# Copies into the keys' input on VectorE, and scatters tied in pairs to their row-number casts: a change to a two-layer perceiver kernel

## The chip, the cores and the metric

The kernel runs on one core of one Trainium2 chip. The core has five engines that run beside each other, each through its own list of instructions in order: TensorE (PE, matmuls; its weight loads are shown as PEld), VectorE (DVE), ScalarE (ACT), GpSimd (POOL) and SyncE (SP, which here issues transfers). [...] Transfers between memory and the core run on 16 DMA engines.

The metric is the device time of one execution in microseconds (us); lower is better. The kernel before takes 2748.53 us, the median of three runs (2745.07 to 2750.08).

## The reference

Sixty-four sequences of 32 tokens of width 256 (`x`) pass two layers. Each layer has a cross attention to a context of 257 tokens per sequence, a self attention, and a feed-forward part; each part adds its result to `x`. All is float32.

```python
def reference(x, ctx, mask, ...):
    x = x + L0_xattn(ctx, layernorm(x), mask, ...)   # queries from ln; keys and values from [xn ; ln], 257 + 32 of them
    x = x + L0_attn(layernorm(x), ...)
    x = x + L0_ffn(layernorm(x), ...)                # mixture of experts
    x = x + L1_xattn(layernorm(x), ctx, ...)
    x = x + L1_attn(layernorm(x), ...)
    x = x + L1_ffn(layernorm(x), ...)
    return x

def L0_ffn(x):                                       # 2048 tokens, 64 experts, 8 for each token
    w, idx = top_k(softmax(x @ gate_w), 8)           # w is then divided by its sum
    pos = place of each choice in its expert's queue # those from 128 on are dropped
    buf[expert, pos] = x                             # one row of 256 numbers for each choice
    out = experts(buf)                               # two matmuls with a silu gate for each expert
    y = sum over the 8 choices of w * out[expert, pos]
    return y + shared_expert(x)
```

In the first cross attention a sequence's keys come from 289 tokens: the first 256 of its context, then the sequence's own 32 tokens (after their layernorm), then the context's last one.

## The kernel before

The 2048 tokens are 16 tiles of 128, four sequences in each. There are three stages. The first, `before`, loops over the 64 sequences: first cross attention, and for each tile, some sequences later, the self attention and the routing (`tail`). The second, `experts`, first finishes the tails that are left and then goes through the 64 experts. The third, `after`, loops over the sequences again for the second layer.

A scheduler places the instructions of DVE, ACT, POOL and SP by priority and by its own estimate of when inputs are there; PE's order is written out by hand: within `tc.manual_schedule(engines={PE})` PE runs its instructions in the order in which the code emits them. The code interleaves the work by Python generators. Each `slot()` in the loop lets every running generator (`tails` for tiles that are done, `fronts` for queries of tiles to come) go on to its next `yield`. A tile has eleven slots. `pause(n)` is n `yield`s. A `yield` sets where PE's instructions go and with which priority the others are emitted; an engine other than PE may still run an instruction from behind a `yield` as early as its inputs allow.

What the change touches:

- `turn(s)` of `CrossFirst` makes `xT`, the transposed 256 x 289 input of a sequence's keys (two buffers that take turns). PE transposes the context (L1235), ACT copies 256 columns out (L1238), and POOL copies the last 33: 32 columns of the sequence's own tokens from `lnT` (L1239) and one of the context's last token from `xlT` (L1240). `keys(s)` multiplies `xT` by the key weights in 16 matmuls (L180, psA<-xT,wk), copies the results to `kT` (L1263 on ACT, L1265 on DVE) and squares them (L1268). `norms` sums the squares on PE (L1280), `scores` multiplies queries and keys (L1320), and DVE scales the scores (L1330).
- `route(t)` is the end of a tile's tail. DVE finds for each token the eight rows of `buf` into which it goes (`far`, float32, with a number outside `buf` for dropped choices), and casts them to int32 (`fi`, L669). POOL then issues eight scatters (L672): scatter k writes the tile's 128 rows of `z` to the rows in column k of `fi`. The scatters are declared free of each other. After each second one the code has a `yield`, but for the last two tiles.

On POOL the scatters share one list with, among others, the products of queries and their norms (L1184), the mask (L1206 to L1208), the weights of the self attention's queries (L565), the count of rows per expert (L653) and the copies into `xT`. The buffer of `z` is one of two that take turns.

Of the kernel before, what the change touches and what calls it, by code (L numbers as in the profile page):

```python
# [19 lines left out]
S = 32  # L20
NB = P // S
J = 257
JK = J + S
# [10 lines left out]
TOPK = 8  # L34
# [56 lines left out]
def pause(n):  # L91

    for _ in range(n):
        yield
# [7 lines left out]
class Kernel:  # L102
# [511 lines left out]
    def route(self, t, gw):  # L614
        nc = self.nc
        z, zT = yield from self.normed(t)
        nc.sync.dma_start(self.zs[t // GT][:, :, t % GT, :], zT)
        ps = self.bank("psA")
        self.product(
            ps[:, : E + 1],  # L620
            [zT[:, k, :] for k in range(2)],
            [gw[:, k, :] for k in range(2)],
        )

        sgt = self.sgate[:, t : t + 1]
        nc.scalar.activation(sgt, ps[:, E : E + 1], AF.Exp, scale=-1.0)
        nc.vector.tensor_scalar(sgt, sgt, 1.0, None, ALU.add)
        nc.vector.reciprocal(sgt, sgt)
        mx = self.small.tile([P, 1], F32, name="mx1")
        sm = self.small.tile([P, 1], F32, name="sm1")  # L630
        nc.vector.tensor_reduce(mx, ps[:, :E], AX.X, ALU.max, negate=True)
        pr = self.wk.tile([P, E], F32, name="pr")
        nc.scalar.activation(pr, ps[:, :E], AF.Exp, bias=mx, accum_out=sm)
        nc.vector.reciprocal(sm, sm)
        nc.vector.tensor_scalar(pr, pr, sm, None, ALU.mult)
        top = self.small.tile([P, TOPK], F32, name="top")
        nc.vector.max(top, pr)
        sel = self.wk.tile([P, E], F32, name="sel")
        nc.vector.match_replace(sel, top, pr, -1.0)
        nc.vector.tensor_scalar(sel, sel, 0.0, None, ALU.is_lt)  # L640
        tot = self.small.tile([P, 1], F32, name="tot")
        nc.vector.tensor_reduce(tot, top, AX.X, ALU.add)
        nc.vector.reciprocal(tot, tot)
        nc.vector.tensor_scalar(pr, pr, tot, None, ALU.mult)

        yield
        yield

        ps = self.bank("psA")
        self.product(ps[:, :E], [self.tri, self.ones], [sel, self.count])  # L650
        kept = self.wk.tile([P, E], F32, name="kept")
        nc.vector.scalar_tensor_tensor(kept, ps[:, :E], float(CAP), sel, ALU.is_lt, ALU.mult)
        nc.gpsimd.tensor_tensor(self.count, self.count, sel, ALU.add)  # L653
        val = self.wk.tile([P, E], F32, name="val")
        nc.vector.tensor_tensor(val, ps[:, :E], self.slot, ALU.add)
        nc.vector.tensor_tensor(val, val, kept, ALU.mult)
        v8 = self.small.tile([P, TOPK], F32, name="v8")
        nc.vector.max(v8, val)
        junk = self.wk.tile([P, E], F32, name="junk")
        for k in range(TOPK):  # L660
            nc.vector.scalar_tensor_tensor(
                junk, val, v8[:, k : k + 1], pr, ALU.is_equal, ALU.mult, accum_out=self.w8[:, t, k : k + 1]
            )
        nc.vector.tensor_copy(self.idx[:, t, :], v8)
        far = self.small.tile([P, TOPK], F32, name="far")
        nc.vector.tensor_scalar(far, v8, 0.0, FAR, ALU.is_equal, ALU.mult)
        nc.vector.tensor_tensor(far, far, v8, ALU.add)
        fi = self.small.tile([P, TOPK], I32, name="fi")
        nc.vector.tensor_copy(fi, far)  # L669

        for k in range(TOPK):
            d = nc.gpsimd.indirect_dma_start(  # L672
                out=self.buf[:, :],
                out_offset=bass.IndirectOffsetOnAxis(ap=fi[:, k : k + 1], axis=0),
                in_=z[:, 0, :],
                in_offset=None,
                bounds_check=E * CAP,
                oob_is_err=False,
            )
            self.tc.declare_no_dep(d.ins, group="scatter", reason="rows differ")  # L680
            self.tc.add_to_no_dep_group("scatter", d.ins)
            if k % 2 and k < TOPK - 1 and t < self.nt - 2:
                yield

    def experts(self, ctx, slot, tails):
        tc, nc, a = self.tc, self.nc, self.a
# [111 lines left out]
        for _ in range(at):  # L798
            next(side)
        turn(0)  # L800
        turn(1)
        inner(0)
        rest = total - at
        for e in range(E):
            weigh(e + AHEAD)
            fetch(e + 3)
            turn(e + 2)
            while (at - total + rest) * E < rest * e:
                next(side)
                at += 1  # L810
            inner(e + 1)
            outer(e)
            if e == AHEAD:
                self.after_weights()
            if e == 2 * AHEAD:
                self.ffnw = self.ffn_weights(self.w2)
# [319 lines left out]
class CrossFirst:  # L1136
# [88 lines left out]
    def turn(self, s):  # L1225

        k, kp = self.k, self.kp
        nc = k.nc
        t, b = divmod(s, NB)
        lnT, cx = self.own[t][1], self.cx[s]  # L1230
        xT = self.xT[s] = kp.tile([P, 2, JK], F32, name="xT")
        ps = k.bank("psT")
        for c in range(2):
            for j in range(2):
                nc.tensor.transpose(  # L1235
                    ps[:, (2 * c + j) * P : (2 * c + j + 1) * P], cx[:, j, c * P : (c + 1) * P], k.ident
                )
        nc.scalar.copy(xT[:, :, : J - 1], ps.rearrange("p (k j) -> p k j", k=2))  # L1238
        nc.gpsimd.tensor_copy(xT[:, :, J - 1 : JK - 1], lnT[:, :, b * S : (b + 1) * S])  # L1239
        nc.gpsimd.tensor_copy(xT[:, :, JK - 1 :], self.xlT[:, :, s : s + 1])  # L1240

    def keys(self, s):

# [291 lines left out]
```

## Time and profile before

| | |
|---|---|
| median of 3 runs | 2748.53 us |
| the profiled execution's own time | 2806.28 us |
| its span, from the first to the last instruction | 2804.2 us |
| mean granted TensorE clock | 0.986 of full speed |
| DMA | 157.05 MB, 56 GB/s over the span |
| POOL's scatters, L672 | 128, 992 ns each, 127.0 us |
| POOL's gathers, L835 | 128, 1027 ns each, 131.4 us |

The profile is one execution, recorded instruction by instruction. Its page gives each engine's busy time, the costliest groups of instructions and what ended the idle time ahead of them. Views of the trace give more: a timeline lists instructions in order of time, with the start and the length in us, the engine, the line, the operation, what is written and what is read, and in brackets the idle time ahead of it and what ended that. "issue" there means that the engine waited for nothing the profile shows. A wait list sums such idle times by pairs. A table of stretches gives the engines' busy times between two points in time.

### The profile page before, as it was taken

The numbers are of one execution on the slowest core, as the hardware profiler recorded it, in microseconds if no ns is written. First come the engines' busy times: TensorE is split into PE (matmuls) and PEld (weight loads), VectorE is DVE, ScalarE is ACT, GpSimd is POOL, SyncE is SP. The second block draws the span as 40 slices with busy tenths as digits, with TensorE's granted clock in tenths as the row PEclk, the third lists the DMA queues.
The fourth block names the chain that finished last, engine by engine and source line by source line (L and its number), as shares of the span: only waits on it lengthen the run. The fifth ranks groups of instructions, "written<-read, shape, count | busy, mean of one in ns | idle before, by whom it ended". The sixth has DMA issues, their size and how long they took to land. (4 is left out here: it accounts for less than half of the span.)

```text
span 2804.2 us, 59449 instructions
## 1 busy us (share of the span) xinstructions
PE 2651.4 (95%) x23642; PEld 1822.2 (65%) x23642; DVE 1736.5 (62%) x4557; ACT 1235.3 (44%) x3474; POOL 543.6 (19%) x644
## 2 busy tenths in 40 slices
PE   6999999999999999999998899899999999999995
PEld 4566656665666566666665578677777777777763
DVE  6565656665676567657755533556666666666664
ACT  4555555555555545555554233333333333333331
POOL 3110122112211221222021300422222222121001
PEclk9999999999999999999999999999999999999997
DMA  8100001101100000000001487221212222221110
GB/s 267 38 16 14 18 31 33 31 18 31 33 28 19 27 22 20 23 17 19 17 9 48 149 292 260 89 62 52 58 48 58 52 58 58 50 58 46 33 33 7
DMA packets 136088, 157.05 MB, mean 56 GB/s; under 512 B 24024, under 2 KB 118979, under 8 KB 135812
## 3 DMA queue, kind: packets, MB, share of 16 engines
q1 hardware_dynamic: 114308, 119.65, 13.9%
q0 software_dynamic: 12288, 25.21, 3.4%
q10 hardware_dynamic: 9216, 8.39, 0.9%
q8 instruction: 187, 3.06, 0.5%
q14 instruction: 89, 0.73, 0.1%
HBM read 121.63 MB, written 37.75 MB: 57 GB/s over the span
## 5 line engine op out<-in xcount | busy, mean ns | idle before, releaser
L180 PE MATMUL psA<-xT,wk 128*128 128x289 f32 x2048 | 525.5, 412 | 18.3 <-issue 13.7
L180 PEld LDWEIGHTS psA<-xT,wk 128*128 128x128 f32 x2048 | 386.5, 191 | 151.3 <-issue 46.5
L835 POOL DMA_INDIRECT y<-oute,idx x128 | 131.4, 1027 | 641.0 <-DVE x L846 466.3
L234 PE MATMUL psY<-at,cx 128*128 128x512 f32 x512 | 237.1, 606 | 0.0
L180 PE MATMUL psY<-xT,qk 128*128 128x257 f32 x1024 | 233.6, 381 | 0.0
L180 PE MATMUL psA<-at,cx 128*128 128x512 f32 x512 | 233.5, 599 | 0.0
L180 PEld LDWEIGHTS psY<-xT,qk 128*128 128x128 f32 x1024 | 189.9, 190 | 25.1
L1421 ACT ACTIVATE sim<-psY,mx 128x257 f32<-128x257 f32 x256 | 120.8, 476 | 148.7 <-DVE mx L1420 147.8
L234 PEld LDWEIGHTS psY<-at,cx 128*128 128x128 f32 x512 | 92.4, 190 | 122.1 <-issue 98.7
L197 ACT ACTIVATE sim<-sim,mx 128x289 f32<-128x289 f32 x256 | 135.4, 532 | 63.2 <-DVE mx L195 63.0
L180 PEld LDWEIGHTS psA<-at,cx 128*128 128x128 f32 x512 | 93.4, 190 | 96.5 <-issue 83.2
L1268 ACT ACTIVATE sq<-kT 128x1156 f32<-128x1156 f32 x128 | 148.5, 1160 | 11.6 <-DVE kT L1265 10.5
L1263 ACT COPY kT<-psA 128x289 f32<-128x289 f32 x256 | 99.3, 388 | 119.7 <-PE psA L180 117.5
L246 ACT COPY yT<-psY 128x512 f32<-128x512 f32 x128 | 68.7, 589 | 188.9 <-PE psY L244 188.9
L1330 DVE TENSOR_TENSOR sim<-psB,sim 128x289 f32<-128x289 f32 x256 | 100.9, 451 | 81.1 <-PE psA L180 28.9
L672 POOL DMA_INDIRECT buf<-z,fi x128 | 127.0, 992 | 96.9 <-DVE fi L669 56.1
L1265 DVE COPY kT<-psA 128x289 f32<-128x289 f32 x256 | 114.0, 449 | 42.7 <-PE psA L180 42.6
L180 PE MATMUL psY<-yT,wv 128*64 128x128 f32 x2048 | 127.9, 277 | 7.3 <-DVE yT L1451 7.3
L1420 DVE TENSOR_REDUCE mx<-psY 128x1 f32<-128x257 f32 x256 | 101.0, 417 | 52.8 <-PE psY L180 52.6
L180 PEld LDWEIGHTS psY<-yT,wv 128*64 128x64 f32 x2048 | 116.6, 138 | 16.3 <-DVE yT L1451 11.2
L186 DVE TENSOR_TENSOR x<-x,psY 128x256 f32<-128x256 f32 (+1 forms) x80 | 29.2, 365 | 154.0 <-PE psY L180 152.4
L180 PE MATMUL psY<-wo,oT 128*128 128x128 f32 (+1 forms) x768 | 124.2, 315 | 0.0
(262 smaller groups left out, 5014.7 us busy)
## 6 DMA issues: line engine op xcount, KB each, us to landing
cx<-in_ctx SPq DMA_DIRECT2D x128, 256.0 KB
we<-in_m_ew SPq DMA_DIRECT2D x64, 384.0 KB
xT<-in_ctxT SPq DMA_DIRECT2D x64, 257.0 KB
buf<-zero SPq DMA_DIRECT2D x32, 256.0 KB
be<-buf SPq DMA_DIRECT2D x64, 128.0 KB
oute<-oe ACTq DMA_DIRECT2D x64, 128.0 KB
mu<-in_mask SPq DMA_DIRECT2D x16, 128.5 KB
x<-in_x SPq DMA_DIRECT2D x16, 128.0 KB
```

Source lines behind the costliest of these rows:

```text
L180: self.nc.tensor.matmul(ps, lhsT=lhs[i], rhs=rhs[i], start=(i == 0), stop=(i == n - 1))
L197: nc.scalar.activation(sim[:, g, :], sim[:, g, :], AF.Exp, bias=mx[:, g : g + 1], accum_out=sm[:, g : g + 1])
L234: nc.tensor.matmul(ps[kc], lhsT=values[i][:, kc * P : (kc + 1) * P], rhs=at[i], start=(i == 0), stop=(i == n - 1 and tail is None),)
L246: nc.any.tensor_copy(yT[:, kc, :, b * S : (b + 1) * S], ps[kc].rearrange("p (h i) -> p h i", h=H))
L672: d = nc.gpsimd.indirect_dma_start(out=self.buf[:, :], out_offset=bass.IndirectOffsetOnAxis(ap=fi[:, k : k + 1], axis=0), in_=z[:, 0, :], ...
L835: nc.gpsimd.indirect_dma_start(out=y, out_offset=None, in_=self.oute[:, :], in_offset=bass.IndirectOffsetOnAxis(ap=self.idx[:, t, k : k + ...
L1263: nc.scalar.copy(kT[:, p, :], ps[:, :JK])
L1265: nc.vector.tensor_copy(kT[:, p, :], ps[:, :JK])
L1268: nc.scalar.activation(sq[p // 4], kT[:, p - 3 : p + 1, :], AF.Square)
L1330: nc.vector.tensor_tensor(sim[:, g, :], ps[i][:, :JK], sim[:, g, :], ALU.mult)
L1420: nc.vector.tensor_reduce(mx[:, g : g + 1], ps[:, :J], AX.X, ALU.max, negate=True)
L1421: nc.scalar.activation(sim[:, g, :], ps[:, :J], AF.Exp, bias=mx[:, g : g + 1], accum_out=sm[:, g : g + 1])
```

## The change

Two things are done. In `turn`, both copies of the last 33 columns of `xT` go from POOL to DVE. In `route`, the one cast of eight row numbers becomes four casts of two for all tiles but the last two, which keep one cast of eight. Ahead of each cast but the first the generator pauses for two slots, and each cast is pinned by `keep_in_program_order`, so that the scheduler may not place it ahead of the DVE instruction that was emitted just before it. Each pair of scatters reads the columns of its own cast. The `yield` behind each pair goes.

```diff
@@ route
         fi = self.small.tile([P, TOPK], I32, name="fi")
-        nc.vector.tensor_copy(fi, far)
-
+
+
+        n = 2 if t < self.nt - 2 else TOPK
         for k in range(TOPK):
+            if k % n == 0:
+                yield from pause(2 if k else 0)
+                self.tc.keep_in_program_order(nc.vector.tensor_copy(fi[:, k : k + n], far[:, k : k + n]))
             d = nc.gpsimd.indirect_dma_start(
...
             self.tc.declare_no_dep(d.ins, group="scatter", reason="rows differ")
             self.tc.add_to_no_dep_group("scatter", d.ins)
-            if k % 2 and k < TOPK - 1 and t < self.nt - 2:
-                yield
@@ turn
         nc.scalar.copy(xT[:, :, : J - 1], ps.rearrange("p (k j) -> p k j", k=2))
-        nc.gpsimd.tensor_copy(xT[:, :, J - 1 : JK - 1], lnT[:, :, b * S : (b + 1) * S])
-        nc.gpsimd.tensor_copy(xT[:, :, JK - 1 :], self.xlT[:, :, s : s + 1])
+        nc.vector.tensor_copy(xT[:, :, J - 1 : JK - 1], lnT[:, :, b * S : (b + 1) * S])
+        nc.vector.tensor_copy(xT[:, :, JK - 1 :], self.xlT[:, :, s : s + 1])
```

## The prediction

> **What bounds the kernel now.** I read the page's busy rows first, then the wait list, then stretches of the timeline, then a table of stretches.
>
> ```profile
> span 2804.2 us, 59449 instructions
> PE 2651.4 (95%) x23642; PEld 1822.2 (65%) x23642; DVE 1736.5 (62%) x4557; ACT 1235.3 (44%) x3474; POOL 543.6 (19%) x644
> ```
>
> TensorE (PE) is the bound: 95% busy, its order written out by hand. In the built programs its order and SyncE's are identical before and after, so the change can only move PE's waits. In the first stage (0 to about 1490 us; tiles of 94.3 us in the steady state) those are few. From the wait list of the whole kernel:
>
> ```profile
> POOL xT L1239 <- PE psA L180: 237.3, 20, 15.4
> ...
> PE psB L1280 <- ACT sq L1268: 10.1, 14, 1.9
> ```
>
> Columns: who <- for whom, us in total, times, longest. GpSimd (POOL) waits for PE to give it the xT buffer; PE is never listed as waiting for POOL's copies. So POOL's 128 copies into xT are early. The pair of copies at 936.06 and 936.23 is read by matmuls that start at 958.68: 22 us of slack.
>
> The loss lies elsewhere. POOL's timeline shows one tile's eight scatters (start, us, what, idle before):
>
> ```profile
> 926.02 1.08 POOL L672 DMA_INDIRECT buf<-z,fi  x1 [4.31 <-DVE fi L669]
> 927.41 0.97 POOL L672 DMA_INDIRECT buf<-z,fi  x1 [0.31 <-issue]
> ...
> 933.81 0.98 POOL L672 DMA_INDIRECT buf<-z,fi  x1 [0.30 <-issue]
> 935.09 0.98 POOL L672 DMA_INDIRECT buf<-z,fi  x1 [0.30 <-issue]
> 936.06 0.26 POOL L1239 COPY xT<-lnT 128x64 f32<-128x64 f32 x1
> ```
>
> The `yield`s of before don't part them: all eight leave in one run of 10.0 us, one per 1.28 us. At the end of the same run, PE, then VectorE (DVE), then ScalarE (ACT):
>
> ```profile
> 933.31 0.40 PE L1320 MATMUL psB<-kT,qTf 64*32 64x289 f32 x1 [0.24 <-issue]
> 933.64 0.61 PE L163 MATMUL psT<-c,z 128*128 128x128 f32 x2
> 934.72 1.13 PE L180 MATMUL psA<-xT,wk 128*128 128x289 f32 x3 [0.47 <-issue]
> 936.15 0.99 PE L180 MATMUL psA<-xT,wk 128*128 128x289 f32 x3 [0.30 <-issue]
> 937.57 1.62 PE L180 MATMUL psA<-xT,wk 128*128 128x289 f32 x6 [0.43 <-issue]
> ...
> 937.62 1.56 DVE L1330 TENSOR_TENSOR sim<-psB,sim 128x289 f32<-128x289 f32 x4 [4.10 <-PE psA L180]
> ...
> 937.90 0.37 ACT L164 COPY zT<-psT 128x256 f32<-128x256 f32 x1 [3.96 <-PE psA L180]
> ```
>
> DVE needs only the psB results that ended at 933.71 and starts 3.9 us later; ACT needs psT of 934.25 and starts 3.65 us later. PE moves in threes, 1.42 us apart. News of finished matmuls travels late until 1.5 us after the last scatter, and PE falters with it. The table of stretches (start:end, length, busy us and count for PE, PEld, DVE, ACT, POOL; clock; DMA):
>
> ```profile
> 926.00:933.20 7.20, 7.06 (x56) 2.79 (x54) 2.67 (x13) 2.90 (x7) 5.66 (x6) 1.00 0.40 130
> 933.20:937.50 4.30, 3.06 (x9) 1.47 (x10) 0.32 (x1) 0.59 (x1) 2.62 (x5) 1.00 0.13 41
> 937.50:944.00 6.50, 6.43 (x27) 4.97 (x27) 5.78 (x11) 2.86 (x10) 4.10 (x3) 1.00 0.00 0
> ```
>
> Nine PE starts in 4.30 us, 27 in the next 6.50, clock full throughout. In the run's first 7.2 us, with six scatters, PE idles 0.14 us. So it is the tail of a long run that hurts.
>
> **The change, part by part.**
>
> *Scatters in pairs.* Tiles 0 to 13 get four 2-column casts instead of one 8-column cast: 14 x 3 = 42 casts more. Each pair of scatters waits for its cast, and each cast is pinned behind the instruction traced before it on DVE. By the order in the built program the parting is uneven: in the steady tile casts 1 and 2 stand two instructions apart (some 1 us), cast 3 just before L564 (951.74 in the old timeline), cast 4 after the key copies of the next block (965 to 966). So 4+2+2, not 2+2+2+2. Four scatters take 5.1 us, inside the harmless 7.2. Tile 12 becomes 2+6, tile 13 4+4; tiles 14 and 15 keep their sixteen.
>
> What a run costs PE: the nine starts of the middle row are one L1320, two transposes and six key matmuls. Key matmuls stand 0.24 us apart in the next row (27 in 6.50); six need 1.45, the other three some 0.35: 1.8 of 4.3 us, so 2.5 lost. Then ACT, made late, is waited for at L1280 some 12 us on: 10.1 us in 14 waits, 0.7 each. 3.2 us x 12 tiles (0 to 11) = 38.4. Tile 12's run ends with a PE wait of 3.9 us (L180 psA<-sw,zT at 1504.66). Together **42 us**. What is late next: nothing PE meets sooner; ACT's xT copy comes 0.1 to 0.8 us ahead of its matmuls as it does in tiles without scatters. If a run of four still leaves a quarter of the stall, 32.
>
> *The copies into xT.* POOL loses 64 of 0.24 us and 64 of 0.20, DVE gains as many. The nearest rows are DVE's 128x64 operations L652 and L655 (0.21 us long, 0.13 apart back to back) and its 128x8 casts (0.16 long, 0.08 apart). So 64 x (0.13 + 0.08) = 13.4 us, and 42 casts x 0.08 = 3.4: 17 us of DVE over fourteen tiles, 1.2 per tile, of which DVE is busy 62 of 94. The built order also hands twelve copies at<-psT (0.6 us) from DVE to ACT: DVE -7, ACT +7. Their cover is DVE's idle third and the 20 us between an xT buffer falling free and its use; on the path between 0 (all covered) and 24 us (17 + 7, none covered). Below 0 I exclude: nothing waited for the old copies. I take 2, since the row above shows PE waiting for nothing but the burst's echo.
>
> *Queues behind the new waits.* On POOL the third pair stands before L565 (qk by sg): at most two scatters, 2.6 us, ahead of transposes that come some 15 us later; L1184 (q by ss) waited 3.4 us for ACT even behind eight scatters. The z buffer that the scatters read is written again at 1013 (one tile after 918.76), the last pair goes at about 966. In tile 13 POOL's L565 started at 1549.08, 2.2 us after its input; with 4+4 it need not wait: 0 to -2, taken as 0. The experts read `buf` only after tile 15's scatters, unchanged.
>
> *A rule against it.* The Trainium skill, "SBUF — State Buffer", sections "SBUF: two separate sides" and "A bandwidth-pool intuition that's wrong (but worth ruling out)", says that a float32 copy from SBUF to SBUF on VectorE locks GpSimd out of a shared port, so that it can't write its descriptors, a transfer of 620 ns then taking 3100. Beside 56 pairs that would be at most 2.5 us each, 140 us of POOL time; on the path still 0, as no one waits for a scatter before the experts. The trace's scatters last 0.97 to 1.41 us, 1.08 where DVE works beside the first: I use that.
>
> Sum, against the profiled execution's own time (2806.3 us, span 2804.2): -42 + 2 = -40, so 2766. The median of the runs shown is 2748.5, 57.8 lower. Taking the same 40 off it: **2709 us**.
>
> **Rivals.**
>
> *B: the stall belongs to the recording.* The skill's "Runtime: NRT & Kernel Launch", section "The ~15µs preamble/postamble breakdown", puts a profile's total a constant 6.2 us over the timed run. Here the gap is 57.8, so 51.6 us of the profile are not in the timed runs, and the runs of scatters account for 42 of just that kind: signals that queue up. By the trace the sum is -40, by that rule about 0. For B: a hidden depth of 7 us before anything shows. Against: slower transfers or other waits could fill the gap as well, since the launch and experts stages hang on DMA. B gives 2748.5 + 2 = 2750.
>
> *C: slower.* In each tile DVE runs back to back from 909 to 928 (18.63 busy of 19.00) while PE never stops (19.00 of 19.00). Two xT copies and two casts go in there, one of them waiting for ACT's lnT (done at 912.2, needed at about 912.6), and an at<-psT goes to ACT. If kT<-psA slips there, the squares (L1268) end after PE reaches L1280, and each added microsecond is PE's. It decides as soon as those squares' slack is under 1 us. Price 17 + 7 = 24 at most, with B's timed runs 2748.5 + 18 = 2766.
>
> *A': half.* Runs of four stall too, or only half of it is in the timed runs: 2729.
>
> **How the numbers follow.** A 0.50 (2709, own range 2698 to 2726), A' 0.11, B 0.23, C 0.16. A measurement of this kernel can tell about 0.2%, 5.5 us, from no change. Faster: A, A' and 0.02 of B, 0.63. Same: most of B, 0.15. Slower: C and the upper part of B, 0.22. Range 2698 to 2762: it leaves out the low end of A (0.06) and the upper half of C (0.09).
>
> **What would show it.** Right: four, two and two scatters per tile; no DVE wait near 4 us at sim<-psB; L1280's waits for ACT sq down from 10.1 to about 2; tiles of 91 us instead of 94.3; profile and median both near -40. B: the profile falls by 40, the median doesn't. C: new PE waits at L1280 or L1320 for DVE or ACT. Wrong: stalls of the same size beside pairs, which would clear the run's length of blame.

## The result, and the profile after

The changed kernel takes 2755.41 us, the median of eight runs (2752.91 to 2762.93). The kernel before, run beside it, takes 2747.59 us (2745.07 to 2750.76). The ratio is 1.003, 95% interval 1.0019 to 1.0042: 7.8 us more, where 40 us less were forecast. The profiled execution of the change takes 2753.39 us, its span is 2751.5 us. So the profile fell by 52.9 us while the timed runs rose by 7.8, and this profile agrees with its timed runs to 2 us, where that of before stood 57.8 us above its own.

The page's span and busy row of the changed kernel (engine, busy us, share of the span, number of instructions):

```profile
span 2751.5 us, 59395 instructions
PE 2627.9 (96%) x23642; PEld 1821.0 (66%) x23642; DVE 1741.4 (63%) x4715; ACT 1242.1 (45%) x3486; POOL 512.7 (19%) x516
```

PE's busy time is 23.5 us shorter for the same 23642 matmuls, so in before's trace part of what counted as busy was time in which matmuls ran late. One tile's scatters on POOL's timeline of the changed kernel (start, us, what, idle before):

```profile
900.34 1.01 POOL L676 DMA_INDIRECT buf<-z,fi  x1 [4.54 <-DVE fi L675]
...
904.25 0.98 POOL L676 DMA_INDIRECT buf<-z,fi  x1 [0.30 <-issue]
921.10 1.07 POOL L676 DMA_INDIRECT buf<-z,fi  x1 [4.72 <-DVE fi L675]
922.48 0.97 POOL L676 DMA_INDIRECT buf<-z,fi  x1 [0.31 <-issue]
936.59 1.01 POOL L676 DMA_INDIRECT buf<-z,fi  x1 [12.38 <-DVE fi L675]
937.90 0.97 POOL L676 DMA_INDIRECT buf<-z,fi  x1 [0.30 <-issue]
```

Four leave together, then two, then two: the 4+2+2 of the forecast. DVE's four-microsecond waits at sim<-psB are gone from the tiles 0 to 11. A steady tile (the time from one tile's matmul to the same matmul of the next tile) takes 90.1 us instead of 94.3. PE's wait for the squares, 10.1 us in 14 times before, has become this in the wait list of the changed kernel (us, times, longest):

```profile
PE psB L1282 <- ACT sq L1270: 5.1, 4, 2.0
```

PE issues the same matmuls in the same order in both, so the two traces can be laid over each other by matmul number. Here is how far the changed kernel is ahead of before's trace (us):

```
matmul     0   2500   5000   7500   10000  12000  14000  23000  23500  end
ahead    0.0    3.5   17.9   29.9    45.2   53.6   59.7   59.8   52.4  52.6
```

It gains about 4 us per tile from the first scatters on, some 6 us more over the last four tiles together (matmuls 12000 to 14000), and then, within the last 60 us, it loses 7.3 us. No term of the sum stood for that. PE's timeline of the changed kernel there:

```profile
2695.38 1.29 PE L1085 MATMUL psB<-kTl,qf 32*32 32x32 f32 x128
2698.54 5.33 PE L180 MATMUL psA<-wl,zT 128*128 128x512 f32 x8 [1.87 <-issue]
...
2711.50 1.42 PE L324 MATMUL psY<-eT,vz 32*32 32x32 f32 x115 [6.76 <-DVE eT L313]
2714.91 0.35 PE L324 MATMUL psY<-eT,vz 32*32 32x32 f32 x13 [2.00 <-issue]
```

and PE's timeline of before at the first of these two places:

```profile
2755.14 1.29 PE L1083 MATMUL psB<-kTl,qf 32*32 32x32 f32 x128
2756.35 3.70 PE L180 MATMUL psA<-wl,zT 128*128 128x512 f32 x8
```

Right after a burst of 128 small matmuls (256 instructions with their weight loads, in 1.3 us) the changed kernel's PE stands still for 1.87 us, waiting for nothing the profile shows, and again for 2.00 us inside the next burst; the eight matmuls after the first gap take 5.33 us instead of 3.70. The table of stretches (start:end, length, busy us and count for PE, PEld, DVE, ACT, POOL; granted clock; DMA) of the changed kernel says why:

```profile
2694.00:2704.00 10.00, 7.09 (x140) 3.90 (x141) 3.36 (x9) 1.26 (x4) 0.73 (x1) 0.83 0.01 2
2704.00:2714.00 10.00, 2.15 (x119) 1.63 (x118) 5.28 (x9) 0.15 (x1) 2.99 (x2) 0.73 0.01 2
```

Before's row for the 10 us from 2753.75, the same work, has the clock at 1.00:

```profile
2753.75:2763.75 10.00, 6.12 (x142) 3.56 (x142) 5.06 (x13) 1.41 (x4) 3.55 (x3) 1.00 0.01 2
```

So two questions are left: why the 4 us per tile that the profile gained are not in the timed runs, and what stops PE in the last 60 us.

### The profile page after: what moved, and what is told of

Its sections match the earlier page's. It is cut to its first block, busy times and chain, and to the rows that moved or that the text cites. A ratio compares the mean times of both kernels' runs of the same rounds, so it can differ in the third digit from the quotient of the medians.

```text
span 2751.5 us, 59395 instructions
## 1 busy us (share of the span) xinstructions
PE 2627.9 (96%) x23642; PEld 1821.0 (66%) x23642; DVE 1741.4 (63%) x4715; ACT 1242.1 (45%) x3486; POOL 512.7 (19%) x516
## 5 line engine op out<-in xcount | busy, mean ns | idle before, releaser
L180 PE MATMUL psA<-xT,wk 128*128 128x289 f32 x2048 | 513.9, 409 | 3.2 <-ACT xT L1240 3.2
L180 PEld LDWEIGHTS psA<-xT,wk 128*128 128x128 f32 x2048 | 384.1, 190 | 123.2 <-ACT xT L1240 11.8
L180 PE MATMUL psA<-at,cx 128*128 128x512 f32 x512 | 233.5, 599 | 0.0
L180 PE MATMUL psY<-xT,qk 128*128 128x257 f32 x1024 | 233.3, 380 | 0.0
L180 PEld LDWEIGHTS psY<-xT,qk 128*128 128x128 f32 x1024 | 189.9, 190 | 24.9
L180 PEld LDWEIGHTS psA<-at,cx 128*128 128x128 f32 x512 | 93.5, 190 | 96.4 <-issue 83.2
L1422 DVE TENSOR_REDUCE mx<-psY 128x1 f32<-128x257 f32 x256 | 101.1, 418 | 53.0 <-PE psY L180 52.9
L180 PE MATMUL psY<-yT,wv 128*64 128x128 f32 x2048 | 126.2, 275 | 7.3 <-DVE yT L1453 7.3
L1441 ACT COPY at<-psT 128x512 f32<-128x512 f32 x117 | 63.7, 588 | 137.9 <-PE psT L1440 69.9
L180 PEld LDWEIGHTS psY<-yT,wv 128*64 128x64 f32 x2048 | 114.9, 137 | 16.3 <-DVE yT L1453 11.2
L180 PE MATMUL psY<-wo,oT 128*128 128x128 f32 (+1 forms) x768 | 124.2, 315 | 0.0
```

What stands on the lines that cost most here:

```text
L180: self.nc.tensor.matmul(ps, lhsT=lhs[i], rhs=rhs[i], start=(i == 0), stop=(i == n - 1))
L1422: nc.vector.tensor_reduce(mx[:, g : g + 1], ps[:, :J], AX.X, ALU.max, negate=True)
L1441: nc.any.tensor_copy(at[:, j, :], ps)
```

## The experiments

In each group the kernel before ran beside the experiments on the same chip.

**First group (chip 15).** *The kernel before, unchanged.*

> The kernel before, unchanged, run again. Theory R (the stall at long runs of scatters exists only in the profiled execution): the profile comes again some 55 to 60 us above the timed runs (2800 to 2808 against 2748), with four-microsecond waits at sim<-psB, and the timed runs are 1.000 of themselves. Rival S (the first profile fell on a disturbed execution, which can happen in any run): this profile lies within some 5 us of the timed runs, with no such waits. Theory G (the 8 us between the two kernels are the clock gate at the end): the granted clock of the timed runs is higher here than the 0.983 to 0.988 listed for the changed kernel, by about 0.002 to 0.003.

Measured: 2803.25 us, and 2803.28 for before beside it (ratio 0.9999, 0.9991 to 1.0007). No theory of the three had this. The profile does agree with the timed runs (2805.34 us), but both are 55 us above the runs first shown. The stall is in this trace; DVE's wait list (who <- for whom, us in total, times, longest):

```profile
DVE sim L1330 <- remote: 26.6, 7, 4.1
...
DVE sim L1330 <- PE psA L180: 24.7, 9, 4.3
```

The timed runs agree with the profile that holds the stall, so on this chip the stall is in the timed runs too. Theory G can't be judged here: the clocks are 0.985 to 0.989, but in runs of 2803 us, not of 2748. It comes back with e5 and e6.

*The copies alone.*

```diff
-        nc.gpsimd.tensor_copy(xT[:, :, J - 1 : JK - 1], lnT[:, :, b * S : (b + 1) * S])
-        nc.gpsimd.tensor_copy(xT[:, :, JK - 1 :], self.xlT[:, :, s : s + 1])
+        nc.vector.tensor_copy(xT[:, :, J - 1 : JK - 1], lnT[:, :, b * S : (b + 1) * S])
+        nc.vector.tensor_copy(xT[:, :, JK - 1 :], self.xlT[:, :, s : s + 1])
```

> Only the 128 copies into xT go to VectorE; casts and scatters as before. Theory R: the profile is again 45 to 60 us above the timed runs, since the long runs of scatters are there. For the 8 us lost: if VectorE's added load costs them (theory D), the timed runs are at 2755 (ratio 1.003); if the casts or the tail cost them (theory T), 2748 (1.000).

Measured: 2809.11 us, ratio 1.0018 (1.001 to 1.0025), so 5.8 us lost, as theory D has it. But the place is not D's. Laid over e1's trace by matmul number, this one is 7.0 us ahead at matmul 23000 and 2.2 behind at the end: the copies cost the first stage nothing, and 9.2 us go in the last 50 us, at the same burst as above.

*The pairs alone*, the copies on GpSimd as before (the casts and pauses of the change, nothing else).

> Only the casts in pairs with pauses; the copies into xT stay on GpSimd. Theory R: the profile agrees with the timed runs within 5 us, as for the whole change, since no run of eight is left in tiles 0 to 11. Theory D: timed 2748 (1.000). Theory T: timed 2755 (1.003).

Measured: 2766.49 us, ratio 0.9872 (0.9857 to 0.9887): 37 us less than before, a saving that T and D, made for runs of 2748 us, did not foresee. No gap in the last 60 us. Steady tiles take 91.08 us.

*The change, with the last four tiles as before.*

```diff
-        n = 2 if t < self.nt - 2 else TOPK
+        n = 2 if t < self.nt - 4 else TOPK
...
+            if n == TOPK and k % 2 and k < TOPK - 1 and t < self.nt - 2:
+                yield
```

> The whole change, but the last four tiles keep one cast of eight columns and the yields of before. If the 8 us are lost in the last tiles, where the casts of tiles 12 and 13 push into the chain that leads to the last scatters and the experts' first fetch (theory T, tail), timed 2748 (1.000) and the profile 10 us above or more, since tile 12 has its run of eight again; if they are lost in the steady tiles, by VectorE's load or by the pairs there, 2755 (1.003).

Measured: 2770.19 us, ratio 0.9888 (0.9873 to 0.9903), with the gap behind the burst in the last 60 us as in the change. Laid over e3's trace by matmul number, it is 3.6 us ahead at matmul 23000 and 4.3 behind at the end. So the last tiles of the first stage are not where the 8 us go. Together: the gaps come with the copies on DVE (e2, e4, the change) and are absent without (before, e3). A reason can be counted in the traces. TensorE's list has 645 instructions that only wait for a semaphore (the signal by which one engine releases another) where GpSimd copies, and 615 where DVE does: 31 fewer at the helper's line L180, through which the matmuls that read `xT` go, and one more at L163. So in the last stage all that follows stands 30 instructions earlier in the list. The instructions are fetched in blocks of about 256: before's list has 47,929, and one of the page's instruction queues makes 187 transfers of 16 KB (the Trainium skill, "Runtime: NRT & Kernel Launch", section "Terms", has the same 16 KiB refill). The last transfer ahead of the burst's end came at 2748.21 in before, 7 us ahead of the burst; in the change it came at 2696.14, inside the burst. All fifteen traces here fall in line: in the four with the gap (the change, e2, e4, e5) that transfer starts 0.7 to 0.8 us into the burst, in the eleven without it 6.9 to 7.1 us ahead of it.

**Second group (chip 10).** *The changed kernel again.*

> The changed kernel, unchanged, run again beside the kernel before. Theory P (the stall at long runs of scatters is there on some chips and absent on others; nothing of it belongs to the recording): the ratio depends on how long before takes here. If before takes 2803 here, the change takes 2755 to 2772, ratio 0.983 to 0.988; if before takes 2748, the change takes 2755, ratio 1.003. Rival R (recording): the change takes 2755 beside any before, and before's time would have to be explained otherwise.

Measured: 2778.14 us beside 2809.87 for before, ratio 0.9894 (0.9877 to 0.9911). The same kernel that lost 7.8 us gains 31.7 on this chip. That fits theory P, which had the ratio depend on before's time; the size is 6 us over its range.

*The change with its blocks put back:* fifteen more transposes ahead of the first two, 30 instructions.

```diff
+        for _ in range(15):
+            nc.tensor.transpose(ps[:, :nb], xl[:, 0, :P], self.ident[:nb, :nb])
```

> The change with 15 more transposes at the very start (30 instructions in TensorE's stream), which bring the boundaries of its 256-instruction fetches in the last stage back to where they lie in the kernel before. Theory F (in the last 60 us the changed kernel's TensorE runs dry in a burst of 256 small instructions because a fetch comes late, idles 2 us, and the clock is halved after it): 6 to 8 us less than e5 in the timed runs, mean clock 0.987 to 0.988 instead of 0.983 to 0.987, and no idle time before psA<-wl,zT in the last 60 us. Rival D (the loss is VectorE's added load or the casts in the first stage): same as e5 or 1 us more.

Measured: 2769.56 us, 8.6 less than e5, with fifteen matmuls and their weight loads more to run; clocks 0.986 to 0.987 instead of 0.983 to 0.986. PE's timeline of e5, then of e6, at the burst:

```profile
2718.43 1.29 PE L1085 MATMUL psB<-kTl,qf 32*32 32x32 f32 x128
2721.78 6.55 PE L180 MATMUL psA<-wl,zT 128*128 128x512 f32 x8 [2.06 <-issue]
```

```profile
2717.51 1.29 PE L1087 MATMUL psB<-kTl,qf 32*32 32x32 f32 x128
2718.73 3.70 PE L180 MATMUL psA<-wl,zT 128*128 128x512 f32 x8
```

The fetch moves from 2719.12, in the middle of the burst, to 2710.59, 7 us ahead of it. The 30 missing waits are still missing here, and DVE still makes the copies; only the place in the list is put back. Theory F holds.

*Before, without the scatters of tiles 0 to 11* (their rows never reach the experts).

```diff
+            if t < self.nt - 4:
+                if k % 2 and k < TOPK - 1:
+                    yield
+                continue
```

> The kernel before without the scatters of tiles 0 to 11 (96 of 128 are left out, so these rows never reach the experts). Theory P: 2743 to 2752 on any chip, since the stall goes with the scatters; so some 50 us below before where before takes 2803, and within 5 us of it where before takes 2748. If before and this differ by less than 15 us on a chip where before takes 2803, the slower chip is slow for another reason than the scatters.

Measured: 2757.25 us, ratio 0.9814 (0.9798 to 0.9831): 52.6 us less. That is 5 us over the range, probably what the scatters left in the last four tiles still cost (e13 below bears on that). The steady tile takes 90.02 us, against 94.1 in e1: the stall costs 4.1 us per tile, where the prediction had 3.2.

*Three steps between the pairs in tiles 0 to 11, with e6's fifteen transposes.*

```diff
-                yield from pause(2 if k else 0)
+                yield from pause((3 if t < self.nt - 4 else 2) if k else 0)
```

> As e6, but with three steps between the pairs instead of two in tiles 0 to 11: in the built order the four casts of a tile then stand apart, so scatters leave in 2+2+2+2 instead of 4+2+2. Where runs of four still cost TensorE 0.9 us per tile (seen as 0.9 us per tile between the traces of e4 and of the changed kernel), this takes 8 to 11 us off e6; where no run costs anything, 0 to 2 us.

Measured: 2769.23 us, no better than e6; a miss. The scatters do leave in 2+2+2+2, and the tile is still 91.07 us. So parting the run of four gains nothing, and the microsecond left per tile (e7: 90.02) is lost elsewhere. e6's trace suggests where. Its POOL timeline, and then PE's:

```profile
579.23 1.01 POOL L678 DMA_INDIRECT buf<-z,fi  x1 [12.37 <-DVE fi L677]
580.55 0.97 POOL L678 DMA_INDIRECT buf<-z,fi  x1 [0.30 <-issue]
```

```profile
580.60 0.52 PE L324 MATMUL psY<-eT,vz 32*32 32x32 f32 x36
581.29 0.26 PE L324 MATMUL psY<-eT,vz 32*32 32x32 f32 x5 [0.17 <-issue]
582.01 0.98 PE L324 MATMUL psY<-eT,vz 32*32 32x32 f32 x87 [0.46 <-issue]
```

A single pair stands beside a burst of 128 small matmuls, and PE stops twice in it: it takes 2.39 us instead of 1.29. Three steps instead of two left this pair where it was (579.27 in e8).

**Third group (chip 4).** *The kernel before once more.*

> The kernel before once more, for the trace of another load. Theory P (chips differ): where it takes 2748, its trace has no waits near 4 us at sim<-psB and tiles of 90.1 us; where it takes 2803 to 2810, it has those waits and tiles of 93.5 to 94.3. Rival R (recording): a trace with those waits and tiles of 94 us beside timed runs of 2748.

Measured: 2804.17 us in a single run, 2805.16 for before beside it, with the stall in the trace. This is a third chip on which before is slow.

*No pair beside such a burst* (with e6's fifteen transposes).

```diff
-                yield from pause(2 if k else 0)
+                yield from pause({2: 3, 4: 4, 6: 2}.get(k, 0) if t < self.nt - 4 else 2 if k else 0)
```

> As e6 (the change with the boundary of the fetches put back), but in tiles 0 to 11 the pairs leave after three, four and two further steps, so that no pair runs beside a burst of 128 small matmuls psY<-eT,vz. Theory B (a scatter slows TensorE only where it issues many small instructions; beside long matmuls a pair costs nothing): where before takes 2803 or more, 0.9 us per tile less than e6, so 9 to 12 us, 2757 to 2760 where e6 takes 2769; the last four tiles keep their loss. Where before takes 2748, the same as e6. Rival: the 0.9 us are paid at whatever stands beside the pair, and the time is that of e6.

Measured: 2757.87 us, ratio 0.9832 (0.9818 to 0.9845), 10.1 us less than e6's kernel beside it. POOL's timeline of e10 and then PE's:

```profile
584.04 1.01 POOL L678 DMA_INDIRECT buf<-z,fi  x1 [18.73 <-DVE fi L677]
585.35 0.98 POOL L678 DMA_INDIRECT buf<-z,fi  x1 [0.30 <-issue]
```

```profile
580.13 1.29 PE L324 MATMUL psY<-eT,vz 32*32 32x32 f32 x128
...
583.05 3.70 PE L234 MATMUL psY<-at,cx 128*128 128x512 f32 x8
```

The burst runs through in 1.29 us, the pair leaves beside eight long matmuls that take 3.70 us, as eight of that size do above at full clock, and the tile takes 89.95 us, no more than without any scatter (e7). Theory B holds.

*e6's kernel again.*

> e6 again beside e10 on the same chip. Where before takes 2803 to 2810: 2766 to 2770, ratio 0.986. Where before takes 2748 (no stall): 2745 to 2749, ratio 0.998 to 1.000, since the late fetch is gone and there is no stall to win back.

Measured: 2767.94 us, ratio 0.9869 (0.9854 to 0.9884), as in the second group.

**Fourth group (chip 5).** *Before, with nothing written by the scatters of tiles 0 to 11.*

```diff
-                bounds_check=E * CAP,
+                bounds_check=E * CAP if t >= self.nt - 4 else 0,
```

> The kernel before with the bound of the scatters of tiles 0 to 11 set to 0: the 96 GpSimd instructions are issued as before, in runs of eight, but every row is out of bounds and none is written (these rows are left out of the result). Theory W (the stall comes from what a scatter sets off outside GpSimd: row writes, and the records of them): 2757 to 2765 where before takes 2803 or more, as without the scatters, and most of the landings recorded. Theory I (the stall comes from GpSimd's running the instruction, its descriptors and its signals): within 10 us of before, 2795 to 2805, with the four-microsecond waits at sim<-psB, and few landings recorded. Between: the part by which it falls is the writes'.

Measured: 2801.78 us, ratio 0.9997 (0.9987 to 1.0008), and the steady tile 94.1 us. Theory I: writing the rows has no part in the stall. POOL's timeline of e12, and DVE's wait behind the run:

```profile
922.63 1.09 POOL L672 DMA_INDIRECT buf<-z,fi  x1 [4.30 <-DVE fi L669]
...
931.67 0.97 POOL L672 DMA_INDIRECT buf<-z,fi  x1 [0.30 <-issue]
```

```profile
934.16 1.56 DVE L1330 TENSOR_TENSOR sim<-psB,sim 128x289 f32<-128x289 f32 x4 [4.02 <-remote]
```

**Fifth group (chip 13).** *e10's kernel again.* By now a second difference between the traces was seen. The page's last part gives the time from a transfer's issue to its landing; the changed kernel's page has it, e5's page of the same program does not. First the one, then the other (what, engine, operation, count, KB each, us to landing):

```profile
be<-buf SPq DMA_DIRECT2D x64, 128.0 KB, 4.3
```

```profile
be<-buf SPq DMA_DIRECT2D x64, 128.0 KB
```

Records of landings are missing. A scatter leaves sixteen of them where none is lost. Counted for the 96 scatters of tiles 0 to 11, beside the steady tile:

```
trace                        landings of 1536   steady tile, us   median of runs, us
before, shown first                     300         94.2          (not known)
e1, before, chip 15                     327         94.1            2803.3
e12, nothing written, chip 5            366         94.1            2801.8
e5, the change, chip 10                 999         91.1            2778.1
e10, chip 4                            1179         89.95           2757.9
the change, first comparison           1527         90.1            2755.4
e13, e10's kernel, chip 13             1527         89.95           2747.7
```

> e10 again, on whatever chip this falls. Theory P (chips differ): sooner or later a chip turns up where before takes 2748; there e10 takes 2745 to 2750, ratio 0.998 to 1.001, and its trace holds nearly all of the landings of its scatters. Rival R (the stall belongs to the fuller way of recording under which these experiments run, and the runs first shown were recorded otherwise): before takes 2800 to 2810 here too, e10 2754 to 2760, ratio 0.983, and a quarter or more of the landings of the scatters in tiles 0 to 11 is missing.

Measured: before takes 2746.24 us here, e13 2747.67, ratio 1.000 (0.9992 to 1.0009). That is theory P's range, and not rival R's 2800 to 2810. So before is met in two kinds of places: it takes 2803 to 2810 us on chips 15, 10, 4 and 5, and 2746 to 2748 on chip 13 and in the first comparison. Below these are called the two kinds of chip, but each chip was met in one group only, so it is not shown that the kind belongs to the chip and not to that one occasion. Before was not traced on chip 13; that it has no stall there is read from its time. Against e10, the same program on chip 4, e13's trace gains nothing in the steady tiles, 2.2 us in the first 1000 matmuls, and 11.6 us between matmuls 12000 and 13000, where the last four tiles' scatters run. (In all it is 16.3 us ahead, the medians 10.2: the run that was traced is e13's fastest.) The clocks of before here, 0.988 to 0.991 against 0.983 to 0.988 of the changed kernel in the first comparison, are in the direction that theory G of e1 forecast.

## Why the prediction was wrong

**The stall and its end: right, for a chip like that of the profile.** The stall goes with the long runs of scatters (e7 takes 52.6 us off by leaving them out), 4+2+2 came out, tiles were forecast at 91 us and take 91.1 on such a chip. There the forecast of the sum, -40, met -31.7 (e5), and -40.3 once the late fetch is out (e6). That the last agrees so closely is partly luck: the stall costs 4.1 us per tile and not 3.2, and some 1.1 of it stays (91.1 against 90.0 without the scatters). "If a run of four still leaves a quarter" had the size of this rest but not its place: parting the run of four gained nothing (e8), and what was left was one pair beside a burst of small matmuls (e10).

**The step that failed is "Taking the same 40 off it".** It moved a saving worked out in a profile of 2806 us to runs of 2748 us, as if both held the stall. The 57.8 us between them were almost the stall itself (e7 finds 52.6 in tiles 0 to 11 alone): the kernel before takes 2746 to 2748 us on one kind of chip and 2803 to 2810 on the other. The profile shown first, with 2806 us, tiles of 94.2 us and 300 landings of 1536, looks like those of the second kind; where it was taken is not known. The runs it was held against are of the first kind, where there was no stall to take away: there the change measures +7.8 us, not -40. Rival B named that gap, gave 2750, and was right that the saving is not in those runs. The skill's constant 6.2 us, on which it leaned, is not what these runs show; they show a profile close to its own timed runs: 2805.3 and 2803.3 in e1, 2753.4 and 2755.4 in the change. B's cause, the recording, isn't needed: in e1 and the other groups the timed runs themselves are slow, and e13, traced as well, has tiles of 89.95 us and nearly all landings. Rival A', half of the saving and 2729, isn't borne out either. That 2755 lies inside the range of 2698 to 2762 is owed to the shares of B and C in it, not to the sum.

**The second failed step is "In the built programs its order and SyncE's are identical before and after, so the change can only move PE's waits".** The matmuls were identical; 30 wait instructions had gone with the copies. No term stood for that. It is 8.6 us on chip 10 (e5 against e6), and the 7.3 us lost in the trace of the first comparison are nearly all of its 7.8; laid over e13's trace, which has neither stall nor late fetch, the change loses 7.5 at the same place. The kernel with the fetch put back was run on a chip without the stall only together with moved pairs (e13), and there the loss is gone: ratio 1.000. The two gaps are only 2 us each; the rest is the clock. In the last 60 us of the changed kernel's trace the clock drops to half right at the end of the first gap, for 3.4 us (2698.45 to 2701.87). The Trainium skill, "TensorE: Matmul & The Clock Gate", "Part 1: The HAM clock gate (the "warmup" mystery)", puts half clock after at least one idle window of some 3.4 us. No single pause here was that long: a pause of 1.69 us, some 1.6 us of small matmuls and a pause of 1.87 us were followed by half clock all the same. Before has the first pause alone at this place and keeps its clock.

**The copies on DVE, taken as 2 us: right.** In the first stage they cost nothing that can be seen (e2 is 7 us ahead at matmul 23000; e13 equals before). Rival C, the squares made late by a fuller DVE, didn't come: PE's waits for them fell to 5.1 us, not to the forecast 2. The rule on the shared port, costed at 0, stays at 0: the scatters take 1000 ns on average, 992 before, and none is slower than 1.04 us of the twelve beside which the moved copies run.

**Open.** Why the two kinds of chip differ, what in the run of a scatter on GpSimd holds up the others, and whether the slower kind would stall in an execution that nothing records: no run here settles these. The records of landings go missing where the stall is, but e10 lacks 357 of 1536 with steady tiles as fast as on chip 13, so the loss alone isn't the stall. e10's kernel is the best of these: 0.983 of before where there is a stall (the change: 0.989), 1.000 where there is none (the change: 1.003).

## What to carry to other kernels

A profile whose own time is far from the median of the timed runs is a profile of something else: find what the gap is made of before moving a saving from one to the other. Where TensorE runs bursts of small matmuls, as here, a change on another engine can cost time by adding or taking away wait instructions, so lay the two traces over each other by matmul number and look for idle time that nothing explains. Scatters from GpSimd were harmless here in pairs beside long matmuls: try that place first.

## What the hardware did that was not expected

- The same program, before, takes 2746 us on chip 13 and 2803 to 2810 us on four others (medians, each chip met once), at granted clocks of 0.984 to 0.991.
- On a chip of the slower kind a pair of scatters costs PE 1.1 us per tile beside 128 small matmuls (steady tiles of 91.0 us in e11, 89.95 in e10), and nothing measurable beside eight of 128x512. In the first comparison's trace of the change the same pair only stretches the burst, from 1.29 to 1.46 us, and the tile takes 90.1 us.
- Whether a scatter writes its rows plays no part in the stall of the long runs (e12).
- Thirty instructions fewer in TensorE's list made the kernel 8.6 us slower, as a fetch of instructions then fell into a burst (e5 against e6).
